# Small norm-parameter loads: one transfer per chunk in the list of later loads, in place of six or nine in one entry

## The chip, the cores and the metric

The kernel runs on one core of one Trainium2 chip (trn2). The metric is device time in microseconds (us), lower is better: the median of the timed executions. The change's time is measured against the kernel before on the same kind of chip. All data are float32.

## The reference

Two transformer layers run one after the other on `x` of 4 x 512 x 320 with a context of 4 x 1601 x 192. Each has self-attention, cross-attention to the context (20 heads of 16) and a gated feed-forward part (320 to 2 x 1280 and back). Each of the three parts begins with a layer norm that has its own scale `g` and bias `b` of 320 elements.

```python
def _ln(x, g, b):
    m = jnp.mean(x, axis=-1, keepdims=True)
    v = jnp.mean(jnp.square(x - m), axis=-1, keepdims=True)
    return (x - m) * jax.lax.rsqrt(v + EPS) * g + b
...
h1 = _ln(x, n1_g, n1_b)
x = _attn(h1, h1, q1, k1, v1, o1_w, o1_b, heads) + x
h2 = _ln(x, n2_g, n2_b)
x = _attn(h2, context, q2, k2, v2, o2_w, o2_b, heads) + x
h3 = _ln(x, n3_g, n3_b)
proj = h3 @ ff_w1 + ff_b1
a, g = jnp.split(proj, 2, axis=-1)
ff = a * jax.nn.gelu(g, approximate=False) @ ff_w2 + ff_b2
return ff + x
```

## The kernel before

**Units and chunks.** Attention is cut into units of one batch element and four heads: 20 units of self-attention and 20 of cross-attention in each layer, and then 4 feed-forward units. I count the attention units of the program from 0 to 79. A unit walks over its keys in chunks of 128: 4 chunks in a self unit, 13 in a cross unit. For every chunk and head, TensorE multiplies keys by queries in two passes (`st<-q,kT`, L1297), and in a third pass subtracts the row maximum (`st<-nrows,ones`, the same line). ScalarE takes the exponential (`pr`, L1307), and TensorE multiplies by the values (`av`, L1323). Beside this, the same rounds of TensorE compute scores of the next unit (`sps`, L1065), whose maxima VectorE reduces (`nmax` and `pm`, L1080).

**The row maxima travel by DMA.** When the maxima of the next unit are complete, `max_end` (from L1125) splits and transposes them on VectorE into `turned` (L1136), and four small transfers of 4 KB each (`nrows<-turned`, L1144) bring them into the rows that the third pass reads. In cross units these four are put on a list of errands and issued one round later. The first `st<-nrows,ones` product of the next unit can't start before all four have landed, and TensorE runs its instructions in order.

**Projections use staging buffers.** `both` (from L887) projects queries and keys of a self unit, ScalarE writes them to `low` (L913), GpSimd splits off `high` (L814, L815), and transfers at L863 move both into `kT` and `q`. There are two buffers `low`. A later unit's write to `low` waits until the transfers out of it are done.

**One DMA queue.** Apart from the first microseconds, every transfer is issued by SyncE (SP in the profile) in program order. An instruction that waits for an engine, or for one of eight semaphores that are used in turn, holds up all that stand behind it. The order of the queue follows from the Python order in which the kernel is written: a planner with rounds, due times and costs decides which projections, norms and errands run in which chunk.

**The list of later loads.** Weights for later parts are kept as closures in `loads`, a queue. At the end of each chunk of an attention unit one entry is taken out and run (`loads.popleft()()` at the end of `main`'s loop). What is left when a feed-forward unit begins is issued at once. The scales and biases of a norm come in columns of 128, 96 or 64 partitions with one element each (`load_columns`, L215 to L218, into `lng` and `lnb`): six transfers for the norms of the two attentions, eight for the third norm. `load_norm` issued them all in one entry, and the third norm's entry, `small`, had the feed-forward bias `b1` (L267) besides, nine in all.

Entries with such groups are put on the list at five places: for the second norm of layer 0 near the start, for the first norm of layer 1 in layer 0's cross-attention, for the third norm at unit 37 of layer 0, for the second norm of layer 1 after the first layer's feed-forward part, and for the third norm again at unit 77. A sixth group, the first norm of layer 0, is loaded at once by `now(load_self(0))` before the first unit.

Of the kernel before, what the change touches and what calls it, by code (L numbers as in the profile page):

```python
# [23 lines left out]
P = 128  # L24
# [11 lines left out]
HK = [(0, 0, P), (1, P, 96), (2, P + 96, 96)]  # L36
# [17 lines left out]
FK = [(0, 0, P), (1, P, P)]  # L54
REST = D - 2 * P
# [20 lines left out]
def kernel(ctx: ExitStack, tc: tile.TileContext, x, context, ws, out):  # L76
# [18 lines left out]
    nc = tc.nc  # L95
# [113 lines left out]
    def load_rows(t, w, chunks):  # L209
        return [  # L210
            lambda k=k, at=at, n=n: dma(out=t[:n, k], in_=w[at : at + n, :].rearrange("(k d) c -> d k c", d=SLOT))
            for k, at, n in chunks
        ]

    def load_columns(t, v, chunks):  # L215
        with nc.allow_non_contiguous_dma(reason="a vector's elements go to partitions"):
            for k, at, n in chunks:
                dma(out=t[:n, k : k + 1], in_=v[at : at + n].rearrange("(k d o) -> d k o", d=SLOT, o=1))  # L218

    def load_row(t, v):  # L220
        dma(out=t, in_=v.rearrange("(o d) -> o d", o=1).to_broadcast([P, D]))
# [5 lines left out]
            load_row(brow[(3 * l + i) % 2], ws[l][("o1_b", "o2_b", "ff_b2")[i]])  # L227

    def load_norm(l, i):
        for t, v in ((lng[i], ws[l][f"n{i + 1}_g"]), (lnb[i], ws[l][f"n{i + 1}_b"])):  # L230
            load_columns(t, v, FK if i == 2 else HK)
            if i == 2:
                for half in range(2):
                    load_columns(t[half * REST :], v, [(2, 2 * P, REST)])

    def load_self(l):
        return [lambda: load_norm(l, 0)] + [
            f for t, n in ((wq1, "q1"), (wk1, "k1"), (wv1, "v1")) for f in load_rows(t, ws[l][n], HK)
        ]

# [8 lines left out]
    def load_cross(l):  # L249
        def rows(t, w):  # L250
            return [
                lambda k=k: dma(out=t[:96, k], in_=w[k * 96 : (k + 1) * 96, :].rearrange("(k d) c -> d k c", d=32))
                for k in range(2)
            ]

        return (
            [lambda: load_norm(l, 1)]
            + load_rows(wq2, ws[l]["q2"], HK)
            + rows(wk2, ws[l]["k2"])
            + rows(wv2, ws[l]["v2"])  # L260
        )

    def load_ff(l):
        def small():
            load_norm(l, 2)
            with nc.allow_non_contiguous_dma(reason="a vector's elements go to partitions"):
                dma(out=b1, in_=ws[l]["ff_b1"].rearrange("(c p) -> p c", p=P))  # L267

        def last_rows(half):
            dma(  # L270
                out=room["w1r"][half * REST : (half + 1) * REST, :],
                in_=ws[l]["ff_w1"][2 * P :, half * FF : (half + 1) * FF].rearrange("(k d) f -> d k f", d=SLOT),
            )

        second = ws[l]["ff_w2"].rearrange("(c p) f -> p c f", p=P)
        return (
            [small],
            [lambda half=half: last_rows(half) for half in range(2)],
            [lambda c=c: dma(out=room["w2"][:, c], in_=second[:, c]) for c in range(NHC)],
        )  # L280
# [78 lines left out]
    at = 0  # L359
# [1174 lines left out]
    def before(u):  # L1534

        if u.kind == "cross" and u.g == 1 and u.b + 1 < B or u.kind == "self" and u.m == EARLY - 2:
            b = u.b + 1 if u.cross else 0
            if u.l == 0:
                load_context(b, 0)
                load_context(b, 1)  # L1540
                if u.cross:
                    add_turned(b, u.start + 46, 6)
        if u.kind == "self" and u.m == 0 and u.l:
            take_rooms(u.l)
        if u.kind == "cross" and u.m == B * G - 1:
            take_weights()
            loads.extend(load_first(u.l, (0, 1, 3)) + load_ff(u.l)[2])
        if u.kind == "cross" and u.m == B * G - 3:
            take_rests()
            small, rests, _ = load_ff(u.l)  # L1550
            loads.extend(small + rests)
        if u.kind == "cross" and u.m == B * G - 2:
            loads.extend(load_first(u.l, (4, 2)))
        if u.kind == "self" and u.m == EARLY:

            if u.l == 0:
                add_turned(0, u.start + 22, 2)
            add_context(0, lambda s: units[u.i - u.m + B * G].own.update(kv=s["cT"]), u.start + 36, yes)

    def after(u):  # L1560

        stage[u.b] += 1
        if u.b == B - 1:
            load_bias(u.l, ("self", "cross", "ff").index(u.kind) + 2)
            if u.kind == "self":
                loads.extend(load_out(u.l, "o2_w"))
            if u.kind == "cross" and u.l + 1 < L:
                loads.extend(load_out(u.l + 1, "o1_w"))
            if u.l + 1 < L:
                if u.kind == "ff":  # L1570
                    loads.extend(load_cross(u.l + 1))
                elif u.kind == "self":
                    loads.extend(load_self(u.l + 1))
# [82 lines left out]
    take_rooms(0)  # L1656
    now(load_x(0))
    now(load_self(0))
    load_bias(0, 0)
    load_bias(0, 1)  # L1660
# [27 lines left out]
    for fs in (load_out(0, "o1_w"), load_x(3), load_cross(0)):  # L1688
        loads.extend(fs)
# [11 lines left out]
    for i, u in enumerate(units):  # L1701
# [10 lines left out]
        for k in (3, SOON, AHEAD):  # L1712
            v = units[i + k] if i + k < len(units) else None
# [32 lines left out]
```

## Time and profile before

| what | value |
| --- | --- |
| median of 3 runs | 2952.94 us (2951.12 to 2955.01) |
| the profiled execution's own time | 2956.35 us |
| its span, first to last instruction | 2954.6 us |
| mean granted TensorE clock | 0.992 |
| TensorE busy, matmuls | 2872.8 us, 97% of the span |
| VectorE, ScalarE, GpSimd busy | 70%, 64%, 44% |
| transfers of L218 (`lng`, `lnb`) | 20 + 20, about 0.6 us of SP each |
| when the six groups start | 2.6, 97.8, 469.8, 1115.1, 1524.8, 2570.6 us |

The profiled execution took 3.41 us more than the median of the runs; 1.75 us of its time lie outside its span. Times in the views are from the start of the span. In a timeline row, the columns are start, busy time, engine, line, operation, output and inputs, shapes and count, and in brackets how long the engine was idle before it and who ended that. SPq is the issuing of SyncE: the time of such a row is that of issuing the transfers and of waits within it, not that of moving the data. PEclk is the granted TensorE clock as a share of full speed.

### The profile page before, as it was taken

The page shows a single profiled execution, that of the slowest core. Times are in us where ns is not written, and L with a number is a line of the kernel's source. Part 1 is how long each engine was busy: PE and PEld are TensorE (multiplying, and loading weights), DVE is VectorE, ACT ScalarE, POOL GpSimd, SP SyncE. Part 2 cuts the span into 40 slices and gives each one's busy share as a digit, 9 for nine tenths or more (in the row PEclk, how much of TensorE's full clock was granted, in tenths as well). Part 3 has the DMA queues.
Part 4 walks back from the last instruction along what each step waited for, and adds up shares of the span by engine and source line. Part 5 has one row for each costly group of instructions (what it writes and reads, how often), then busy time and mean ns, then how long its engine had stood idle before and what let it go on. Part 6 is the DMA issues. An engine that isn't in the chain of part 4 may idle for free.

```text
span 2954.6 us, 84378 instructions
## 1 busy us (share of the span) xinstructions
PE 2872.8 (97%) x35018; PEld 1514.5 (51%) x35018; DVE 2060.8 (70%) x4031; ACT 1890.9 (64%) x3754; POOL 1290.0 (44%) x1409
## 2 busy tenths in 40 slices
PE   8999999999999999999999999999999999999999
PEld 4445554555555555355554555555555555544554
DVE  7767887888888888323258778888888888873221
ACT  3766677887877878601138676778778788783000
POOL 3556344555545545211215663455455464461110
PEclk8999999999999999999999999999999999999999
DMA  4443224222232222210113342222221121222000
GB/s 105 107 121 101 71 65 107 55 71 71 53 89 57 52 62 62 70 31 11 42 43 82 98 105 68 63 62 54 55 65 46 50 71 43 58 54 79 20 22 14
DMA packets 186543, 188.70 MB, mean 64 GB/s; under 512 B 69668, under 2 KB 137264, under 8 KB 186160
## 3 DMA queue, kind: packets, MB, share of 16 engines
q1 hardware_dynamic: 185368, 182.11, 24.3%
q8 instruction: 276, 4.52, 0.6%
q10 hardware_dynamic: 760, 1.18, 0.2%
q14 instruction: 107, 0.88, 0.1%
q0 software_dynamic: 32, 0.00, 0.0%
HBM read 55.76 MB, written 29.36 MB: 29 GB/s over the span
## 4 chain that ended last, share of the span: by engine, by line
PE 81%; DVE 13%; DMA 2%; ACT 1%; SPq 1%; issue 1%; POOL 1%; ACTq 0%; POOLq 0%; DVEq 0%
PE av L1323 22%; PE st L1297 16%; PE fps L1408 9%; DVE pm L1080 8%; PE sps L1065 6%; PE yps L1515 6%; PE vps L1026 5%; PE ops L1223 3%; PE kps L962 3%; PE qkps L897 3%; DVE nmax L1080 3%; PE fps L1468 2%; PE qps L938 2%; PE sps L1092 1%; ACT pr L1307 1%
## 5 line engine op out<-in xcount | busy, mean ns | idle before, releaser
L1307 ACT ACTIVATE pr<-st 128x512 f32<-128x512 f32 (+1 forms) x2720 | 1404.8, 603 | 403.0 <-PE st L1297 367.8
L1080 DVE TENSOR_REDUCE pm<-sps 128x1 f32<-128x512 f32 x1920 | 1188.1, 681 | 149.9 <-PE sps L1065 138.1
L1343 POOL TENSOR_TENSOR o<-o,vo 128x512 f32<-128x512 f32 x576 | 740.2, 1285 | 966.7 <-ACT vo L1342 950.1
L1065 PE MATMUL sps<-kT,q 32*128 32x512 f32 x4800 | 868.6, 430 | 11.6 <-DMA q<-low 3.1
L1297 PE MATMUL st<-q,kT 32*128 32x512 f32 (+1 forms) x5120 | 782.9, 421 | 2.2 <-ACT low L913 1.9
L1323 PE MATMUL av<-pr,vals 128*32 128x512 f32 (+1 forms) x5440 | 737.2, 608 | 45.3 <-ACT pr L1307 9.7
L1297 PEld LDWEIGHTS st<-q,kT 32*128 32x128 f32 (+1 forms) x5120 | 417.4, 180 | 289.7 <-issue 122.0
L1297 PE MATMUL st<-nrows,ones 32*128 32x512 f32 (+1 forms) x2720 | 539.8, 399 | 12.0 <-DMA nrows<-turned 12.0
L1065 PEld LDWEIGHTS sps<-kT,q 32*128 32x128 f32 x4800 | 426.6, 184 | 91.7 <-ACT pr L1307 13.4
L1080 DVE TENSOR_REDUCE nmax<-sps 128x1 f32<-128x512 f32 x640 | 396.3, 681 | 101.8 <-PE sps L1065 97.1
L1342 ACT COPY vo<-av 128x512 f32<-128x512 f32 x576 | 352.6, 612 | 25.2 <-PE av L1323 21.1
L1479 ACT ACTIVATE gl<-fps,b 128x512 f32<-128x512 f32 x80 | 54.8, 687 | 414.2 <-PE fps L1468 303.3
L1408 PE MATMUL fps<-hT,w 128*128 128x512 f32 x640 | 283.0, 597 | 0.0
L1323 PEld LDWEIGHTS av<-pr,vals 128*32 128x32 f32 (+1 forms) x5440 | 111.2, 108 | 320.6 <-DVE pm L1080 181.3
L1297 PEld LDWEIGHTS st<-nrows,ones 32*128 32x128 f32 (+1 forms) x2720 | 245.2, 180 | 37.5 <-issue 9.9
L1480 DVE SCALAR_TENSOR_TENSOR hid<-fps,b,gl 128x512 f32<-128x512 f32 x80 | 59.7, 748 | 240.9 <-ACT gl L1479 238.9
L1408 PEld LDWEIGHTS fps<-hT,w 128*128 128x128 f32 x640 | 119.3, 190 | 155.3 <-issue 152.8
L1515 PE MATMUL yps<-w,hid 128*128 128x320 f32 x640 | 176.3, 435 | 0.1
L1515 PEld LDWEIGHTS yps<-w,hid 128*128 128x128 f32 x640 | 120.4, 190 | 56.5 <-ACT gl L1479 5.3
L1223 PEld LDWEIGHTS ops<-wo,aT 112*32 112x32 f32 (+1 forms) x3072 | 98.2, 110 | 58.3 <-issue 40.5
L1223 PE MATMUL ops<-wo,aT 112*32 112x160 f32 (+1 forms) x3072 | 125.0, 301 | 0.7 <-POOL aT L1205 0.7
L514 POOL TENSOR_SCALAR root<-root 128x4 f32<-128x4 f32 x22 | 5.2, 237 | 263.3 <-DVE root L508 262.6
(91 smaller groups left out, 2494.5 us busy)
## 6 DMA issues: line engine op xcount, KB each, us to landing
kT<-stages SPq DMA_DIRECT2D x160, 200.2 KB
oway<-o SPq DMA_DIRECT2D x80, 256.0 KB
q<-high SPq DMA_DIRECT2D x160, 64.0 KB
q<-low SPq DMA_DIRECT2D x160, 64.0 KB
kT<-high SPq DMA_DIRECT2D x60, 128.0 KB
q<-high SPq DMA_DIRECT2D x60, 128.0 KB
kT<-low SPq DMA_DIRECT2D x57, 128.0 KB
aT<-oway SPq DMA_DIRECT2D x32, 224.0 KB
```

The lines of the kernel that those rows point to most:

```text
L897: nc.tensor.matmul(ps[f : f + m, :w], lhsT=wqk[:n, k, f // GD, column : column + m], rhs=first.hT[:n, k, at : at + w], start=(k == 0), sto ...
L1026: nc.tensor.matmul(ps[f : f + m, :w], lhsT=u.kvT[:n, k, at + f : at + f + m], rhs=wv[:n, k, h0 * DH : h1 * DH], start=(k == 0), stop=(k == ...
L1065: nc.tensor.matmul(ps, lhsT=u.q[j * SLOT : (j + 1) * SLOT, e, t * P : (t + 1) * P], rhs=u.kT[j * SLOT : (j + 1) * SLOT, u.k0 + s * 512 : u ...
L1080: nc.vector.tensor_reduce(to[:, j : j + 1], ps, AX.X, ALU.max)
L1223: nc.tensor.matmul(ps[f : f + m, : D // 2], lhsT=aT[:n, k, f * NQ + t * SLOT : f * NQ + t * SLOT + m], rhs=wo[:n, k, cols], start=(k == 0) ...
L1297: nc.tensor.matmul(own[0][:r, :], lhsT=ones[rows, :r] if e == 2 else u.keys(rows, c), rhs=u.rows[rows, :] if e == 2 else u.q[rows, e, :], ...
L1307: nc.scalar.activation(p[:r], own[0][:r], AF.Exp)
L1323: nc.tensor.matmul(ps[j * SLOT : (j + 1) * SLOT, :], lhsT=columns_of[:r, head : head + SLOT], rhs=pr.pop((c, j))[:r, :], start=True, stop= ...
L1342: nc.scalar.copy(vo, ps)
L1343: nc.gpsimd.tensor_tensor(u.o, u.o, vo, ALU.add)
L1408: nc.tensor.matmul(ps, lhsT=w1[:, k, i * FF + c * P : i * FF + (c + 1) * P], rhs=natural(u.hT[:, k]), start=start, stop=stop,)
L1515: nc.tensor.matmul(ps[:, :D], lhsT=hid[c][:, t * P : (t + 1) * P], rhs=w2[:, c, :], start=(c == 0), stop=(c == NHC - 1),)
```

## The change

`load_columns` and `load_norm` no longer issue transfers but return lists of closures, one for each column. `load_self` and `load_cross` put these six entries ahead of the weights, and `load_ff` returns eight entries and a ninth for `b1`. So each group takes six or nine chunks in place of one, and every entry behind it on the list moves five or eight chunks later. No transfer is added or left out: SP has 1749 transfers in both. Line numbers behind the edited functions grow by up to 4.

```diff
     def load_columns(t, v, chunks):
-        with nc.allow_non_contiguous_dma(reason="a vector's elements go to partitions"):
-            for k, at, n in chunks:
+        def column(k, at, n):
+            with nc.allow_non_contiguous_dma(reason="a vector's elements go to partitions"):
                 dma(out=t[:n, k : k + 1], in_=v[at : at + n].rearrange("(k d o) -> d k o", d=SLOT, o=1))
 
+        return [lambda c=c: column(*c) for c in chunks]
...
     def load_norm(l, i):
+        fs = []
         for t, v in ((lng[i], ws[l][f"n{i + 1}_g"]), (lnb[i], ws[l][f"n{i + 1}_b"])):
-            load_columns(t, v, FK if i == 2 else HK)
+            fs += load_columns(t, v, FK if i == 2 else HK)
             if i == 2:
                 for half in range(2):
-                    load_columns(t[half * REST :], v, [(2, 2 * P, REST)])
+                    fs += load_columns(t[half * REST :], v, [(2, 2 * P, REST)])
+        return fs
 
     def load_self(l):
-        return [lambda: load_norm(l, 0)] + [
+        return load_norm(l, 0) + [
             f for t, n in ((wq1, "q1"), (wk1, "k1"), (wv1, "v1")) for f in load_rows(t, ws[l][n], HK)
         ]
...
         return (
-            [lambda: load_norm(l, 1)]
+            load_norm(l, 1)
             + load_rows(wq2, ws[l]["q2"], HK)
             + rows(wk2, ws[l]["k2"])
             + rows(wv2, ws[l]["v2"])
         )
...
     def load_ff(l):
-        def small():
-            load_norm(l, 2)
+        def biases():
             with nc.allow_non_contiguous_dma(reason="a vector's elements go to partitions"):
                 dma(out=b1, in_=ws[l]["ff_b1"].rearrange("(c p) -> p c", p=P))
...
         return (
-            [small],
+            load_norm(l, 2) + [biases],
```

On TensorE, VectorE, ScalarE and GpSimd every instruction keeps its place. Only SP's queue is reordered. Three places of it follow, in the order of the program.

The first is SP in self-attention of layer 0, near 98 us of the profile: `lng_121` and `lnb_124` are the second norm's parameters, `q_104` is the query buffer of a coming unit, `wq_113` the query weights of cross-attention. Before:

```order
L863 DMA q_104<-high 64x512
L863 DMA q_104<-low 64x512
L218 DMA lng_121<-in_L_xattn_n_g_dram 128x1x1
L218 DMA lng_121<-in_L_xattn_n_g_dram 96x1x1 x2
L218 DMA lnb_124<-in_L_xattn_n_b_dram 128x1x1
L218 DMA lnb_124<-in_L_xattn_n_b_dram 96x1x1 x2
L863 DMA q_104<-high 64x512
L863 DMA q_104<-low 64x512
L211 DMA wq_113<-in_L_xattn_q_dram 128x1x320
L1164 DMA oway_130<-o 4x32x512
L1144 DMA nrows_97<-turned 8x4x32 x4
```

And now:

```order
L866 DMA q_104<-high 64x512
L866 DMA q_104<-low 64x512
L218 DMA lng_121<-in_L_xattn_n_g_dram 128x1x1
L866 DMA q_104<-high 64x512
L866 DMA q_104<-low 64x512
L218 DMA lng_121<-in_L_xattn_n_g_dram 96x1x1
L1167 DMA oway_130<-o 4x32x512
L1147 DMA nrows_97<-turned 8x4x32 x4
L218 DMA lng_121<-in_L_xattn_n_g_dram 96x1x1
L218 DMA lnb_124<-in_L_xattn_n_b_dram 128x1x1
```

The second pair of `q_104` stands behind one small load, not six, and `wq_113` is no longer ahead of the four `nrows`.

The second place is SP in cross-attention of layer 0, near 470 us: `lng_120` and `lnb_123` are the first norm's parameters for layer 1, `nrows_97` the row maxima of unit 22. Before:

```order
L243 DMA wo<-in_L_xattn_o_w_dram 96x1x320
L752 DMA ctxT_127<-stages 768x1x64
L218 DMA lng_120<-in_L_xattn_n_g_dram 128x1x1
L218 DMA lng_120<-in_L_xattn_n_g_dram 96x1x1 x2
L218 DMA lnb_123<-in_L_xattn_n_b_dram 128x1x1
L218 DMA lnb_123<-in_L_xattn_n_b_dram 96x1x1 x2
L1144 DMA nrows_97<-turned 8x4x32 x4
L211 DMA wqk<-in_L_xattn_q_dram 128x1x320
L211 DMA wqk<-in_L_xattn_q_dram 96x1x320 x2
```

And now:

```order
L247 DMA wo<-in_L_xattn_o_w_dram 96x1x320
L755 DMA ctxT_127<-stages 768x1x64
L218 DMA lng_120<-in_L_xattn_n_g_dram 128x1x1
L1147 DMA nrows_97<-turned 8x4x32 x4
L218 DMA lng_120<-in_L_xattn_n_g_dram 96x1x1 x2
L218 DMA lnb_123<-in_L_xattn_n_b_dram 128x1x1
L1167 DMA oway_130<-o 4x32x512
L218 DMA lnb_123<-in_L_xattn_n_b_dram 96x1x1
```

One small load, not six, stands ahead of the four `nrows`.

The third place is SP in unit 37 of layer 0, from 1115 us on (the same in layer 1 from 2571 us): `w1r` are feed-forward weights, two transfers of 320 KB, and `nrows_97` the maxima of unit 38. Before:

```order
L218 DMA lnb_125<-in_L_xattn_n_b_dram 64x1x1 x2
L267 DMA b_117<-in_L_xattn_ff_b_dram 128x20x1
L1164 DMA oway_131<-o 4x32x512
L863 DMA kT_101<-stages 64x801 x4
L270 DMA w1r<-in_L_xattn_ff_w_dram 64x1x1280 x2
L863 DMA q_103<-high 64x256
L863 DMA q_103<-low 64x256
L863 DMA q_103<-high 64x256
L863 DMA q_103<-low 64x256
```

And now:

```order
L218 DMA lnb_125<-in_L_xattn_n_b_dram 64x1x1
L866 DMA q_103<-high 64x256
L866 DMA q_103<-low 64x256
L866 DMA q_103<-high 64x256
L866 DMA q_103<-low 64x256
L218 DMA lnb_125<-in_L_xattn_n_b_dram 64x1x1
L270 DMA b_117<-in_L_xattn_ff_b_dram 128x20x1
L273 DMA w1r<-in_L_xattn_ff_w_dram 64x1x1280 x2
L1147 DMA nrows_97<-turned 8x4x32 x4
```

The two `w1r` now stand directly ahead of the four `nrows` of unit 38; before, eight transfers of `q_103` lay between.

## The prediction

> **What bounds the kernel now.** I read the page first, to see which engine the whole time hangs on.
>
> ```profile
> PE 2872.8 (97%) x35018; PEld 1514.5 (51%) x35018; DVE 2060.8 (70%) x4031; ACT 1890.9 (64%) x3754; POOL 1290.0 (44%) x1409
> PE 81%; DVE 13%; DMA 2%; ACT 1%; SPq 1%; issue 1%; POOL 1%; ACTq 0%; POOLq 0%; DVEq 0%
> ```
>
> TensorE is busy for 97%, and the second row, the chain that ended last, is TensorE's for 81%. A change of the SP queue can only touch what TensorE waits for. So the next view is TensorE's waits, and in it one row is about transfers that L218 can hold up (columns: total us, times, longest us).
>
> ```profile
> PE st L1297 <- DMA nrows<-turned: 12.0, 10, 3.0
> ```
>
> The longest of these ten waits, 3.0 us, is at 478.78 us; TensorE's, VectorE's and SP's timelines show what led to it.
>
> ```profile
> 468.87 0.21 DVE L1136 STREAM_TRANSPOSE turned<-nmax 128x32 f32<-128x32 f32 x1
> ...
> 469.84 3.03 SPq L218 DMA_DIRECT2D lng<-in_L_xattn_n_g_dram  x3
> 472.92 1.89 SPq L218 DMA_DIRECT2D lnb<-in_L_xattn_n_b_dram  x3
> 474.90 2.67 SPq L1144 DMA_DIRECT2D nrows<-turned  x4
> ...
> 478.78 0.49 PE L1297 MATMUL st<-nrows,ones 32*128 32x512 f32 x2 [3.03 <-DMA nrows<-turned]
> ```
>
> The maxima of unit 22 were ready on VectorE at 469.08. SP was then issuing the six norm loads, from 469.84 to 474.81, and came to `nrows` only at 474.90. TensorE would have gone on at 478.78 - 3.03 = 475.75.
>
> The stall has a second price. The next view has TensorE's work and its granted clock in stretches that I cut at the clock's own changes (columns: length, busy time of PE, PEld, DVE, ACT, POOL, then PEclk, DMA share, GB/s).
>
> ```profile
> 169.10:172.50 3.40, 1.73 (x16) 0.46 (x16) 3.27 (x9) 1.77 (x4) 3.14 (x6) 1.00 0.56 147
> 476.31:479.72 3.41, 0.94 (x16) 0.59 (x18) 0.79 (x2) 0.44 (x1) 0.00 (x0) 1.00 0.18 50
> 479.72:486.55 6.83, 6.83 (x55) 2.88 (x56) 4.63 (x9) 4.26 (x9) 1.27 (x1) 0.50 0.26 61
> 1643.67:1647.08 3.41, 1.35 (x24) 0.67 (x20) 1.62 (x3) 0.89 (x3) 3.41 (x3) 1.00 0.46 119
> 1647.08:1650.49 3.41, 3.41 (x36) 1.76 (x38) 1.58 (x3) 2.13 (x5) 2.83 (x10) 0.50 0.86 224
> ```
>
> Behind a stretch of 3.41 us in which TensorE worked for only 0.94 us, the clock was 0.50 for 6.83 us, and TensorE was busy in all of it: 3.41 us of work at full clock took twice that. The rows near 1645 us show the same for 1.35 us of work, with one slow stretch. The row at 169 us, 1.73 us of work, was followed by full clock.
>
> A smaller stall lies behind the first group. These are rows of the chain of waits near 100 us, then ScalarE's and TensorE's timeline there.
>
> ```profile
> 97.75 0.60 SPq L218
> ...
> 101.01 0.60 SPq L218
> 101.65 1.18 SPq L863
> 102.88 2.38 DMA q<-low
> ...
> 105.37 0.47 ACT L913 ACTIVATE low<-qkps,scales 128x256 f32<-128x256 f32 x1 [1.87 <-DMA q<-low]
> 105.89 0.49 PE L1065 MATMUL sps<-kT,q 32*128 32x512 f32 x1 [0.88 <-ACT low L913]
> ```
>
> The six loads are on the chain: `q<-low` behind them empties a buffer that ScalarE wants to write, and TensorE waits 0.88 us for ScalarE.
>
> **The change part by part.** One small load costs SP about 0.60 us, 0.64 with the gap to the next:
>
> ```profile
> L218 SPq DMA_DIRECT2D lng<-in_L_xattn_n_g_dram x20: 592/602/1691, 2.6 to 2573.1; - x20
> ```
>
> *The group at 470 us.* One load, not six, stands ahead of `nrows`, which so move up by five issues, 5 x 0.64 = 3.2 us. The three loads at 469.84 took 3.03 us, not 1.9, so 1.1 us of the queue's own hold-up lies there; I leave it in front of `nrows`. The first `nrows` starts at 469.84 + 0.65 = 470.5, and the last is issued by 474.90 + 2.67 - 3.2 = 474.3. It lands 1.66 us after its issue begins, by this row of the chain:
>
> ```profile
> 476.99 1.66 DMA nrows<-turned
> ```
>
> So 476.99 - 3.2 + 1.66 = 475.4, ahead of the 475.75 at which TensorE is ready. The bounds: all 3.03 us saved, or, should the queue hold `nrows` another 1.1 us, 475.4 + 1.1 - 475.75 = 0.8 us left and 2.2 saved. I take 3.03, by the rows of the same queue. Even with 0.8 us idle, the stretch would keep more than the 1.73 us of work that was enough at 169 us, so the slow clock goes too: 6.83 x 0.5 = 3.41 us. Between nothing and 3.41, I take 3.41.
>
> *The group at 98 us.* `q<-low` stands behind one small load, and is issued about 3.2 us earlier, so its buffer is free at about 102 us, before ScalarE is ready at 105.37 - 1.87 = 103.5. The 0.88 us go. Lower bound 0: another operand could come next. I take 0.88.
>
> *The groups at 1115, 1525 and 2571 us* cost nothing now, and nothing is gained. Two rows of SP's timeline and one of the chain of waits show what covers them:
>
> ```profile
> 1120.21 0.59 SPq L267 DMA_DIRECT2D b<-in_L_xattn_ff_b_dram  x1
> 1123.13 0.61 SPq L1164 DMA_DIRECT2D oway<-o  x1
> ...
> 1519.05 12.05 DVE nmax L1080 x20
> ```
>
> At 1115 us the queue is done at 1120.80 and next waits for GpSimd's `o` until 1123.13, 2.3 us of cover; at 1525 us TensorE is held by VectorE's maxima for 12.05 us. The group at 2.6 us is issued by `now` and stays as it is.
>
> *Later weights.* Every weight behind a group comes five or eight chunks later. Two rows of the chain, a chunk apart, and the first users by source line and tile:
>
> ```profile
> 1112.68 1.07 PE av L1323 x8
> 1115.87 1.06 PE av L1323 x8
> ...
> L962 PE MATMUL kps<-w x1280: 330/332/357, 217.4 to 2362.9; 96*32 96x200 f32 x138, 96*32 96x201 f32 x45
> L938 PE MATMUL qps<-hT,wq x960: 377/379/382, 272.6 to 2592.3; 96*32 96x256 f32 x128, 128*32 128x256 f32 x64
> L1468 PE MATMUL fps<-hT,w1r x320: 589/589/693, 1232.0 to 2928.9; 64*128 64x512 f32 x160
> ```
>
> A chunk takes 3.2 us, so the delay is 16 to 26 us. The group at 98 us and the seven weight loads behind it are 13 entries, which end near 97.75 + 13 x 3.2 = 139 us; the key and query weights are first used at 217 and 273 us, `w1r` at 1232 us. Cost 0, since some 80 us cover it; without that cover, TensorE would wait for a weight as it did for `q<-low` above, some 2.4 us. SP issues as many transfers as before.
>
> The sum: 3.03 + 3.41 + 0.88 = 7.32 us. In the profiled execution's own terms 2956.35 - 7.32 = 2949.0. The median of the runs is 3.41 us below that execution; the same sum from it gives 2952.94 - 7.32 = **2945.6 us**.
>
> **The rivals.**
>
> *The slow clock isn't there to save.* The profiled execution lies 3.41 us above the median, just what 6.83 us at half clock cost. Other executions may cut the same 3.03 us of idleness into two stretches, each with more than 1.73 us of work, and keep full clock. Then only 3.03 + 0.88 = 3.91 us go: 2949.0 us. For it: the range of the three runs, 3.9 us, has room for such a spell. Against it: 3.03 us idle leave little room in two stretches of 3.41. The Trainium skill, page "TensorE: Matmul & The Clock Gate", section "Part 1: The HAM clock gate", says that half rate follows at least one idle window of about 3.4 us, and that the window runs free of the kernel's start. Read strictly, a gap of 3.03 us never fills a window, and the saving would be that of this rival; the row at 476.31, with 0.94 us of work and half clock behind it, differs, while a free phase fits a spell that is there in some runs only.
>
> *The stall only moves.* `nrows` could still be late at 478 us, if it is the queue's hold-up and not the issue count that delays it. Its price is at least the 0.8 us above; for a full stall the hold-up would have to grow from 1.1 to 4.3 us. Then 2952.9 - 0.9 = 2952 us.
>
> *Slower: `w1r` ahead of `nrows`.* In both layers, 640 KB now go directly ahead of the maxima of units 38 and 78.
>
> ```profile
> 1128.64 1.75 SPq L270 DMA_DIRECT2D w1r<-in_L_xattn_ff_w_dram  x2
> ...
> 1144.87 0.59 SPq L863 DMA_DIRECT2D q<-low  x1
> 1158.11 2.65 SPq L1144 DMA_DIRECT2D nrows<-turned  x4
> ...
> 1163.23 0.39 PE L1297 MATMUL st<-nrows,ones 32*128 32x512 f32 x1
> ```
>
> At the 224 GB/s of the row at 1647 us, 640 KB take 2.9 us, and their issue 1.75. If both fall directly ahead of 1158.11, `nrows` land 4.7 us later than now (issued by 1158.11 + 2.65 = 1160.8, landed 1.1 us behind the end of the last issue at 1161.9), that is at 1166.6, and TensorE, which uses them at 1163.23, waits 3.3 us and then loses 3.41 at half clock: 6.7 per layer, 13.4 in all, net +6.1 us, 2959.0. It decides from the point where SP comes to `w1r` later than 1158.1 - 4.7 = 1153.4. Against it: the small loads and `w1r` wait for no engine; SP is free from 1144.87 + 0.59 = 1145.5 to 1158.1. Three more small issues, 1.9 us, and `w1r` are done at 1149.2, and the data by 1152.1, 6 us ahead of need.
>
> **How the numbers follow.** The forecast has 0.56, the missing slow clock 0.25, the moved stall 0.07, the slower case 0.12. A measurement of this kernel can tell about 0.2%, 5.9 us. The forecast and little else is faster by more: 0.58. The slower case gives 0.12. The rest, 0.30, is within. The range: down to 2942.2, where one more slow spell of 3.41 us is gone; up to 2952.4, which takes in the case without the slow clock and a spell of 3.41 elsewhere.
>
> **What would show it.** In the profile of the changed kernel: `nrows` issued at 470 to 474 us and no wait of TensorE for them near 478; the clock at 1.00 from 476 to 487; no wait of ScalarE for `q<-low` near 105 us; `w1r` issued near 1140 to 1150 us and again in layer 1, with the `nrows` of units 38 and 78 not waited for. The prediction is wrong if a new stall of 2 us or more with a half clock behind it stands anywhere in place of the one at 478, or if `nrows` there are still late.

## The result and the profile after

| what | before | after |
| --- | --- | --- |
| median, 15 executions each | 2953.49 us (2950.87 to 2956.47) | 2946.70 us (2943.98 to 2953.61) |
| ratio | | 0.9982, interval 0.9976 to 0.9989 |
| span of the profiled execution | 2954.6 us | 2948.5 us |
| mean granted TensorE clock in it | 0.992 | 0.993 |

The change makes the kernel faster, by 3 to 7 us by the interval; the ratio stands for 5.3 us, the medians lie 6.8 us apart. The prediction was 2945.6 us, and the median is 1.1 us above it. First the page of the profile after, engine totals and the chain that ended last:

```profile
PE 2871.7 (97%) x35018; PEld 1513.0 (51%) x35018; DVE 2060.2 (70%) x4031; ACT 1890.3 (64%) x3754; POOL 1287.7 (44%) x1409
PE 81%; DVE 13%; ACT 1%; DMA 1%; issue 1%; POOL 1%; SPq 1%; POOLq 0%; ACTq 0%; DVEq 0%
```

TensorE is still the bound, with the same shares. In the list of TensorE's waits, the row that the prediction went by (total us, times, longest) is now:

```profile
PE st L1300 <- DMA nrows<-turned: 9.4, 9, 2.4
```

It was 12.0, 10, 3.0. One wait is gone, the longest. The timelines of VectorE, SP and TensorE show the place, unit 22. Its maxima come 3.6 us earlier in the span than before, by what happened ahead of this place, and its product 6.9 us earlier:

```profile
465.23 0.21 DVE L1139 STREAM_TRANSPOSE turned<-nmax 128x32 f32<-128x32 f32 x1
...
466.56 0.65 SPq L218 DMA_DIRECT2D lng<-in_L_xattn_n_g_dram  x1
467.31 2.69 SPq L1147 DMA_DIRECT2D nrows<-turned  x4
470.04 1.32 SPq L218 DMA_DIRECT2D lng<-in_L_xattn_n_g_dram  x2
...
471.92 0.39 PE L1300 MATMUL st<-nrows,ones 32*128 32x512 f32 x2
```

The maxima are turned at 465.23 + 0.21 = 465.44, one small load is issued, and `nrows` follow at 467.31, 1.9 us behind the maxima; before it was 474.90 - 469.08 = 5.8 us. (The prediction wanted to see `nrows` issued at 470 to 474 us; by the clock of the span they are earlier, because the whole unit is.) The last of the four is issued at 470.00, and TensorE uses them at 471.92 without a wait (no bracket behind the row). The other small loads come after `nrows`. The windows around the place (length, then busy time of PE, PEld, DVE, ACT, POOL, then the granted clock) hold full clock throughout:

```profile
464.00:476.00 12.00, 11.79 (x176) 6.27 (x168) 10.60 (x24) 9.82 (x21) 4.90 (x4) 1.00 0.24 55
476.00:487.00 11.00, 10.16 (x152) 5.27 (x156) 10.82 (x26) 8.36 (x19) 6.92 (x13) 1.00 0.54 133
```

The second place that the prediction named is the group at 98 us:

```profile
98.24 0.60 SPq L218 DMA_DIRECT2D lng<-in_L_xattn_n_g_dram  x1
98.89 0.61 SPq L866 DMA_DIRECT2D q<-high  x1
99.54 0.59 SPq L866 DMA_DIRECT2D q<-low  x1
...
104.42 0.47 ACT L916 ACTIVATE low<-qkps,scales 128x256 f32<-128x256 f32 x1 [0.44 <-PE qkps L900]
```

`q<-low` is issued at 99.54, 3.3 us earlier than before (102.88). ScalarE waits only 0.44 us, and for TensorE's product, not for a buffer. TensorE's wait of 0.88 us there is gone.

Third, the place of the slower rival, `w1r` ahead of the `nrows` of unit 38:

```profile
1140.33 2.23 SPq L273 DMA_DIRECT2D w1r<-in_L_xattn_ff_w_dram  x2
1151.23 2.63 SPq L1147 DMA_DIRECT2D nrows<-turned  x4
...
1156.37 0.39 PE L1300 MATMUL st<-nrows,ones 32*128 32x512 f32 x1
```

`w1r` is issued by 1142.6, 8.7 us ahead of `nrows`, and nobody waits for those. In layer 1 it is 2597.42 and 2607.59, the same.

**Where the time of the span went.** These are the stretches at half clock from 100 us to the last microsecond of the span, from the clock's own records (start and length in us):

| before | after |
| --- | --- |
| 203.2 (6.83), 479.7 (6.83), 1531.0 (6.83), 1647.1 (3.41) | 174.0 (3.41), 1064.9 (6.83), 1525.7 (3.41), 1648.5 (3.41) |
| 23.90 us in all | 17.06 us in all |

6.84 us less at half clock is 3.4 us of time, out of the 6.1 us between the spans. But it isn't the same list with one entry taken out: 479.7 is gone, and so is 203.2, while 174.0 and 1064.9 are new. (TensorE's waits ahead of these two, 1.85 and 1.53 us, are under the 2 us that the prediction named as a sign of being wrong.) Unit 8's wait for `nrows`, 1.88 us before and 1.85 after, brought half clock in the profile after only, at 174.0. So one profile beside another can't tell how large the clock's part is; the timed executions can, as below.

### The profile page after: what moved, and what is told of

Same layout as the page of the kernel before. It is cut to its first block, busy times and chain, and to the rows that moved or that the text cites. A ratio compares the mean times of both kernels' runs of the same rounds, so it can differ in the third digit from the quotient of the medians.

```text
span 2948.5 us, 84388 instructions
## 1 busy us (share of the span) xinstructions
PE 2871.7 (97%) x35018; PEld 1513.0 (51%) x35018; DVE 2060.2 (70%) x4031; ACT 1890.3 (64%) x3754; POOL 1287.7 (44%) x1409
## 4 chain that ended last, share of the span: by engine, by line
PE 81%; DVE 13%; ACT 1%; DMA 1%; issue 1%; POOL 1%; SPq 1%; POOLq 0%; ACTq 0%; DVEq 0%
PE av L1326 22%; PE st L1300 16%; PE fps L1411 10%; DVE pm L1083 8%; PE sps L1068 6%; PE yps L1518 6%; PE vps L1029 5%; PE ops L1226 3%; PE kps L965 3%; PE qkps L900 3%; DVE nmax L1083 3%; PE fps L1471 2%; PE qps L941 2%; PE sps L1095 1%; ACT pr L1310 1%
## 5 line engine op out<-in xcount | busy, mean ns | idle before, releaser
L1345 ACT COPY vo<-av 128x512 f32<-128x512 f32 x576 | 354.1, 615 | 23.9 <-PE av L1326 20.1
```

Of the source, the lines that this page charges most:

```text
L1345: nc.scalar.copy(vo, ps)
```

## The experiments

Eight runs, four in each of two sittings; seven are new kernels, the eighth is the changed kernel again. In both sittings the kernel before ran beside them: median 2953.38 us (35 executions) and 2953.28 us (30).

Each timed execution comes with its span and its mean granted clock, so that its time can be split: (1 - clock) x span is what the half clock cost, the rest is time less that. (The clock is given to 0.001, 2.9 us, in each execution, which averages out; idle time at half clock counts too. So does half clock in the first 100 us: there the ten traces have from 10.2 to 27.3 us of it, 5 to 14 us in this column, ahead of the first place at which any of these kernels differs.) Means with their standard errors, in us:

| kernel | executions | median | ratio to before (interval) | cost of half clock | rest |
| --- | --- | --- | --- | --- | --- |
| before | 65 | 2953.3 | | 20.5 (0.4) | 2933.4 (0.3) |
| after (15 and 10 of the last experiment) | 25 | 2946.6 | 0.9982, 0.9974 | 17.0 (0.8) | 2930.1 (0.4) |
| only the first norm's loads one by one | 11 | 2946.80 | 0.9981 (0.9972 to 0.9991) | 16.6 (1.1) | 2931.4 (0.8) |
| only the second norm's | 11 | 2953.19 | 1.0000 (0.9991 to 1.0009) | 22.3 (1.0) | 2931.4 (0.8) |
| only the third norm's | 12 | 2954.24 | 1.0009 (0.9998 to 1.0019) | 22.4 (1.6) | 2933.5 (0.5) |
| groups kept, rows first | 11 | 2950.16 | 0.9987 (0.9978 to 0.9997) | 19.6 (1.2) | 2930.9 (0.5) |
| group at 470 us doubled | 10 | 2960.60 | 1.0026 (1.0017 to 1.0035) | 25.2 (1.1) | 2935.7 (0.6) |
| group at 470 us in two halves | 11 | 2949.24 | 0.9987 (0.9979 to 0.9996) | 17.2 (0.9) | 2932.4 (0.8) |
| after, and rows first | 9 | 2946.25 | 0.9976 (0.9967 to 0.9986) | 15.7 (0.7) | 2930.7 (0.5) |
| after again | 10 | 2946.15 | 0.9974 (0.9965 to 0.9984) | 15.3 (1.4) | 2930.8 (0.7) |

The two columns don't follow the wait at unit 22 kernel by kernel, so I use them only where many executions stand behind them. Against the kernel before of the same sitting, the group in two halves has no wait there and yet a rest only 0.3 us lower (standard error 0.9); the kernel with only the second norm's loads one by one keeps the wait and has a rest 2.6 us lower (0.9); with the rows first, half clock costs only 0.8 us less (1.3).

### One kind of group alone

The changed kernel with two of the three groups put back into one entry. For the first norm alone:

```diff
-            load_norm(l, 1)
+            [lambda: now(load_norm(l, 1))]
...
-            load_norm(l, 2) + [biases],
+            [lambda: now(load_norm(l, 2) + [biases])],
```

> Only the group for the first norm of layer 1 (at 470 us) is spread; the other groups stay in one entry. My theory (the group held nrows of unit 22 back): TensorE's wait of 3.0 us at 478 is gone, and with it the slow clock that followed; 3.0 us less if that slow clock is only in some executions, up to 6.4 less if in all, so a ratio of 0.9978 to 0.9990. Rival (spreading relieves the queue at every group alike): about a fifth to a quarter of the change's 6.8 us, 1.5 us less, ratio 0.9995.

Measured: 2946.80 us, which is the whole gain as far as the intervals tell, though SP's order differs from the kernel before only between 470 and 525 us. TensorE's timeline and a window show no wait for the rows of unit 22 and full clock behind it; the wait near 105 us is still there, 0.95 us.

```profile
474.24 0.39 PE L1300 MATMUL st<-nrows,ones 32*128 32x512 f32 x2
```

```profile
468.00:488.00 20.00, 19.04 (x281) 9.79 (x284) 18.78 (x41) 15.85 (x34) 10.24 (x13) 1.00 0.38 89
```

For the second norm alone, the group at 98 us, the first and third are put back in the same way:

> Only the groups for the second norms (at 98 and 1525 us) are spread. Theory: ScalarE's wait for q<-low and TensorE's 0.88 us behind it at 105 us go, nothing else; the wait of 3.0 us at 478 stays; ratio 0.9997, between 0.9992 and 1.0003. Rival (relief at every group alike): two fifths of 6.8 us, 2.7 us less, ratio 0.9991, and it would need a second place of gain near 1525 us.

Measured: 2953.19 us, no gain that can be told from nothing (the interval reaches 2.7 us to both sides). ScalarE doesn't wait for `q<-low` near 105 us, as in the kernel after, so the small stall is gone, and what it cost is too little to be seen in the time. The stall of unit 22 is there in full; TensorE's timeline and two windows of this kernel:

```profile
475.77 0.79 PE L1300 MATMUL st<-nrows,ones 32*128 32x512 f32 x2 [3.34 <-DMA nrows<-turned]
```

```profile
471.49:474.90 3.41, 0.94 (x16) 0.30 (x8) 1.90 (x5) 0.33 (x1) 1.16 (x1) 1.00 0.08 4
474.90:485.14 10.24, 9.37 (x72) 4.15 (x76) 4.80 (x9) 4.92 (x10) 1.27 (x1) 0.50 0.24 61
```

Half clock lasts 10.24 us here, 9.37 of them with TensorE at work: a price of 4.7 us, not 3.4.

For the third norm alone:

> Only the groups for the third norms (at 1115 and 2571 us) are spread, so w1r stands directly ahead of nrows of units 38 and 78. Theory: no change within 0.5 us, ratio 1.0000 and between 0.9994 and 1.0006, nrows issued and landed as before. Rival (w1r delays nrows): TensorE waits 3 us for nrows near 1163 and 2619 us, 6 us or more slower. Rival (relief at every group alike): 2.7 us less.

Measured: 2954.24 us, no gain, and the wait at unit 22 is 2.86 us with 10.24 us at half clock. `w1r` are issued some 8.5 us ahead of the `nrows` of units 38 and 78, and TensorE doesn't wait for those, near 1163 and 2624 us of this span, so the rival with the late rows is out. That nothing changes within 0.5 us can't be told: the interval reaches from 0.6 us less to 5.6 us more, and four of the twelve executions took over 2959 us, against two of the 35 of the kernel before. The profile is one of these (span 2959.4). Windows near 2105 us:

```profile
2104.60:2108.01 3.41, 1.31 (x20) 0.71 (x20) 1.49 (x4) 0.98 (x3) 1.26 (x1) 1.00 0.03 6
2108.01:2114.84 6.83, 6.83 (x52) 2.75 (x48) 4.16 (x7) 4.06 (x8) 2.52 (x2) 0.50 0.07 10
```

Unit 66's wait for `nrows`, 1.39 us before, was 2.10 us here, and half clock followed. SP's order there is the same as in the kernel before, but the four `nrows` took it longer, 2.99 us before and 3.91 us here:

```profile
2102.64 2.99 SPq L1144 DMA_DIRECT2D nrows<-turned  x4
...
2101.74 3.91 SPq L1147 DMA_DIRECT2D nrows<-turned  x4
```

So this stretch isn't one that the edit reordered. Whether long executions are commoner in this kernel than in the kernel before stays open.

### The groups kept, the rows first

The kernel before, but in cross units no entry of the list is taken in the chunk between the maxima and the issue of their rows:

```diff
-            if loads:
+            if loads and (last or not (u.cross and nxt.cross) or c != u.nch - 3):
                 loads.popleft()()
```

> The kernel before, with all groups still in one entry, but no entry of the list is taken in the chunk between the maxima of a cross unit and the issue of their rows, so that the six loads at 470 us come behind nrows of unit 22. Theory: the same gain as spreading the group at 470 us alone, 3.0 to 6.4 us less, ratio 0.9978 to 0.9990, and no wait at 478. Rival (spreading itself helps): no gain, ratio 1.0000.

Measured: 2950.16 us. The six loads are still issued in one go, only behind `nrows`, and TensorE neither waits at unit 22 nor slows down near it. SP's timeline:

```profile
469.60 2.67 SPq L1144 DMA_DIRECT2D nrows<-turned  x4
472.31 1.94 SPq L218 DMA_DIRECT2D lng<-in_L_xattn_n_g_dram  x3
474.30 1.88 SPq L218 DMA_DIRECT2D lnb<-in_L_xattn_n_b_dram  x3
```

So the wait hangs on the place in the queue, not on the grouping, and the gain, 3.2 us by the medians, is at the low end of what I expected. That the median lies 3.4 us above that of the first experiment isn't explained with certainty, since the intervals overlap; but its profile shows a price of the group at 98 us that the prediction didn't have. SP's, ScalarE's and TensorE's timeline, then two windows:

```profile
98.89 2.64 SPq L218 DMA_DIRECT2D lnb<-in_L_xattn_n_b_dram  x3
...
104.71 0.47 ACT L913 ACTIVATE low<-qkps,scales 128x256 f32<-128x256 f32 x1 [3.02 <-DMA q<-low]
...
105.23 0.50 PE L1065 MATMUL sps<-kT,q 32*128 32x512 f32 x1 [2.05 <-ACT low L913]
```

```profile
102.25:105.66 3.41, 1.36 (x20) 0.72 (x16) 1.29 (x2) 0.95 (x3) 3.16 (x5) 1.00 0.58 134
105.66:109.07 3.41, 3.41 (x29) 1.01 (x28) 1.29 (x2) 2.05 (x5) 0.35 (x1) 0.50 0.35 104
```

The queue held up the group itself by some 0.7 us (2.64 in place of 1.9), TensorE waited 2.05 us in place of 0.88, and 3.41 us at half clock came behind it. It is one execution; whether it accounts for the median isn't shown.

### The count of loads ahead of the rows

Two kernels change only the number of small loads between the maxima of unit 22 and `nrows`. In one it is twelve, six of them into tiles that nothing reads:

```diff
-        return [lambda: load_norm(l, 0)] + [
+        def group():
+            load_norm(l, 0)
+            if l:
+                for t, n in zip(spare, ("n1_g", "n1_b")):
+                    load_columns(t, ws[l][n], HK)
+
+        return [group] + [
```

> The kernel before, with the group at 470 us doubled: six more small loads of the same size behind the six, into spare tiles that nothing reads. Theory (nrows of unit 22 stand behind the group in one queue, 0.64 us per transfer): nrows are issued 6 x 0.64 = 3.8 us later, at about 478.7, TensorE's wait at 478 grows from 3.0 to about 6.9 us, and the granted clock is 0.50 behind it for one spell of 6.83 us or more. Time by the idle part alone +3.8 us, about 2957; with a longer half clock up to +7 us, about 2960. Rival (the queue's own hold-up of 1.1 us and not the count sets the delay): the wait grows by less than 1.5 us and the time stays within 2 us of before. Rival (TensorE's wait is filled by work that would be idle elsewhere): the wait grows but the time doesn't.

In the other it is three, scales and biases being two entries:

```diff
-        return [lambda: load_norm(l, 0)] + [
+        pair = ((lng[0], "n1_g"), (lnb[0], "n1_b"))
+        return [lambda t=t, n=n: load_columns(t, ws[l][n], HK) for t, n in pair] + [
```

> The kernel before, with the group at 470 us in two entries of three loads (the scales in one chunk, the biases in the next), so that three small loads stand ahead of nrows of unit 22 in place of six or one. Theory (count of issues): nrows move up by 3 x 0.64 = 1.9 us, TensorE's wait at 478 falls from 3.0 to about 1.1 us. TensorE then works for about 0.9 + 1.9 = 2.8 us of a stretch of 3.41 us, more than the 1.73 us that kept full clock at 169 us, so no half clock stands near 480 us: 1.9 + 3.4 = 5.3 us less than before, about 2948. If the loss to the clock only follows the length of the wait, it is 1.9 us and a part of 3.4, about 2950. Rival (what delays nrows is the queue's hold-up of 1.1 us within the first three loads and a wait for a semaphore): the wait stays at 2 us or more with half clock behind it, 2952.

Measured with twelve: 2960.60 us. SP's and TensorE's timeline, then the windows:

```profile
471.54 1.94 SPq L219 DMA_DIRECT2D lng<-in_L_xattn_n_g_dram  x3
473.53 2.66 SPq L219 DMA_DIRECT2D lnb<-in_L_xattn_n_b_dram  x3
476.24 1.88 SPq L219 DMA_DIRECT2D spare<-in_L_xattn_n_g_dram  x3
478.17 1.88 SPq L219 DMA_DIRECT2D spare<-in_L_xattn_n_b_dram  x3
480.14 2.67 SPq L1151 DMA_DIRECT2D nrows<-turned  x4
...
484.13 0.80 PE L1304 MATMUL st<-nrows,ones 32*128 32x512 f32 x2 [6.57 <-DMA nrows<-turned]
```

```profile
480.92:484.13 3.21, 0.00 (x1) 0.03 (x1) 0.00 (x0) 0.00 (x0) 0.00 (x0) 0.50 0.05 5
484.13:491.16 7.03, 7.03 (x56) 3.36 (x56) 3.26 (x7) 3.28 (x7) 1.27 (x1) 0.50 0.21 62
```

The wait grew from 3.03 to 6.57 us, by 3.5 for six issues, as the count says (3.8). Half clock behind it with TensorE at work is 7.03 us against 6.83: no more than before. By this the time should rise by some 3.6 us; it rose by 7.3. Of the other 3.7 us the table puts 3.1 on half clock (25.2 - 20.5 = 4.7, less 1.6 for the 3.21 idle us above); where in the span that lies stays open, and the half clock of the first 100 us is in that column too.

With three: 2949.24 us. SP's and TensorE's timeline:

```profile
467.68 1.94 SPq L218 DMA_DIRECT2D lng<-in_L_xattn_n_g_dram  x3
469.72 2.67 SPq L1145 DMA_DIRECT2D nrows<-turned  x4
...
473.35 0.39 PE L1298 MATMUL st<-q,kT 32*128 32x512 f32 x1
...
473.58 0.45 PE L1298 MATMUL st<-nrows,ones 32*128 32x512 f32 x2
```

I had expected a wait of 1.1 us; there is none. Three loads took 1.94 us here, where the first three of the kernel before took 3.03: the hold-up of 1.1 us didn't come. The clock near 480 us is full. For 1, 3, 6 and 12 loads ahead of `nrows` the wait is 0, 0, 3.03 and 6.57 us, and the medians are 2946.2, 2949.2, 2953.3 and 2960.6. The step between the first two isn't one of this wait: the kernel with one load is the whole change, and the intervals of the two overlap. With no wait and no half clock left here, 3.03 + 3.41 = 6.4 us should have gone; 4.0 us did, and why the rest didn't stays open.

### The change and the rows first; the change again

The changed kernel with the condition of the rows-first kernel added:

> The changed kernel, and besides no entry of the list of later loads is taken in the chunk of a cross unit between its row maxima and the issue of their rows. Theory: the stall at 478 is gone already, so nothing is left for the second edit: the time of the changed kernel, 2946 to 2948, no wait for nrows of unit 22, and the wait at 105 us absent as in the changed kernel. Rival (weights ahead of nrows delay them elsewhere too): another 1 to 4 us less, 2943 to 2946, with smaller waits for nrows of units 8 and 48.

Measured: 2946.25 us, beside 2946.15 for the changed kernel in the same sitting. Its profile has no wait for `nrows` longer than 1.1 us, and still the time isn't another. None of the kernels tried is faster than the change.

> The changed kernel once more, for a second profile and more executions with their clocks. Theory (the idle part and the half clock behind 478 us are both gone in every execution): the time less what the clock cost, that is time - (1 - clock) x span, lies 4 us under the kernel before, and the mean clock is higher by about 0.001, which is 3 us; together 6 to 7 us, about 2946.5, with no wait and no half clock near 478 us in the profile. Rival (the half clock behind 478 us is there in some executions only): the mean clock is that of the kernel before within 0.0003, and 4 us in all are saved, about 2949.5.

Measured: 2946.15 us, the time that I expected; but against the kernel before of the same sitting half clock costs 5.4 us less (standard error 1.5) and the rest is 2.0 us lower (0.8), where I expected 3 and 4. The rival, with no gain from the clock, is out; the split is not the one expected. SP's timeline and a window at unit 22 show what the first profile showed:

```profile
465.57 0.65 SPq L218 DMA_DIRECT2D lng<-in_L_xattn_n_g_dram  x1
466.32 2.83 SPq L1147 DMA_DIRECT2D nrows<-turned  x4
```

```profile
464.00:487.00 23.00, 21.98 (x324) 11.46 (x320) 21.69 (x50) 18.20 (x39) 12.19 (x18) 1.00 0.36 88
```

The half clock near 1065 us, which was new in the first profile after, is not in this one.

## Why the prediction was right

**The wait at 478 us (3.03 us): right.** Place and size held. `nrows` start 1.9 us behind the maxima, and no wait is left. In four kernels with six or more loads ahead of `nrows` the wait is there (3.03, 3.34, 2.86 and 6.57 us); in six with three, one or none it isn't. Where the prediction was too careful: it left the queue's hold-up of 1.1 us in front of `nrows` and had them ready 0.35 us before need; they moved up by 3.9 us against the maxima, not 3.2. The hold-up isn't tied to these loads; it is 1.1, 0.7 or nothing for the same transfers in different executions. Its cause is open. It isn't a wait for one of the eight semaphores: in the trace of the kernel before, the transfer that had used the held load's semaphore last had landed some 3 us before that load's issue began.

**The half clock behind it (3.41 us): the mechanism was right, against the rival to which I gave the next largest chance; the size came from one execution.** In all four traces with the full wait, half clock stands there (6.83, 10.24, 10.24 and 10.24 us); in none of the six without it is there any from 464 to 487 us. With TensorE at work in 6.83, 9.37, 9.56 and 7.03 us of it, the price was 3.4, 4.7, 4.8 and 3.5 us; the prediction had sized it by the lowest of these. Over all executions the table gives 20.5 - 17.0 = 3.5 us for the clock (standard error 0.9) and 2933.4 - 2930.1 = 3.3 us for the rest (0.5), where the prediction had 3.41 and 3.91. The rival would have had 0 and 3.91. That both parts agree this well with the forecast is partly luck, since the last experiment alone gives 5.4 and 2.0. The Trainium skill, page "TensorE: Matmul & The Clock Gate", section "Part 1: The HAM clock gate", asks for at least one idle window of about 3.4 us; the traces differ, since half clock came behind a window with 0.94 us of work. That the window runs free agrees: half clock began 0.94 us after TensorE went on in the kernel before, and 0.87 us before it in the second experiment.

**The wait at 105 us (0.88 us): its mechanism is shown, its gain isn't.** The wait is in all six traces that keep that group (0.74 to 0.95 us, and 2.05 once) and in none of the four that spread it. Done alone it moves the time by nothing that can be measured.

**The groups at 1115, 1525 and 2571 us, and the later weights: no gain, as forecast.** The third norm's loads alone gave 1.0009, and TensorE waits for no weight in any of the ten traces. (The 2.4 us that the prediction gave for such a wait are the time of the transfer `q<-low`; TensorE's own wait there was 0.88.)

**The slower rival fell at its own condition.** It needed `w1r` to be issued less than 4.7 us ahead of `nrows`; they are 8.7 us ahead, as the prediction had argued from the time in which SP is free.

**A bound that was reasoned badly.** The prediction took 1.73 us of work in a stretch of 3.41 as enough for full clock, from one row. It isn't a threshold. Three windows of the profile after:

```profile
1645.10:1648.51 3.41, 2.22 (x32) 1.06 (x28) 1.64 (x5) 1.26 (x3) 3.41 (x6) 1.00 0.32 103
1648.51:1651.92 3.41, 3.41 (x28) 1.27 (x32) 1.16 (x2) 1.75 (x4) 1.18 (x2) 0.50 0.21 40
1634.86:1638.27 3.41, 1.73 (x16) 0.46 (x16) 3.06 (x5) 1.71 (x4) 3.20 (x5) 1.00 0.32 90
```

A stretch with 2.22 us of work was followed by half clock, one with 1.73 us wasn't. It did no harm because the wait went altogether; with 0.8 us of it left, the 3.41 us would not have been safe.

**The total.** The forecast had 7.32 us less than a median of three executions, and 6.8 us came, from 15. Of the 7.32, the 0.88 us can't be seen in any measured time, and the 3.41 us come from one spell, so a forecast within 1.1 us is closer than its terms are known.

## What to carry to other kernels

In a queue that issues in program order, what counted here was how many transfers stood between the moment a small, urgent transfer became ready and its own issue; a batch of tiny loads cost 0.64 us each there in this kernel, and nothing that could be measured at the places where no engine waited for what stood behind it. Spreading the batch and moving it behind the urgent transfer both removed the wait. A gap of 3 us on TensorE was paid for about twice here, once idle and once at half clock, so the longest gaps are the ones to look at first.

## What the runs showed of the hardware

After the first 100 us, half clock came in lengths of 3.41, 6.83 and 10.24 us, on a grid of 3.41 us whose phase differs between executions. I counted TensorE's work in the windows of that grid in all ten traces. After a window with at most 1.50 us of work, half clock followed 16 times of 16; after one with 1.60 to 2.40 us, 11 times of about 30. So a stall of 1 to 2 us costs half clock in some executions and not in others. It is one source of the scatter around a median: in 35 executions of the kernel before the mean clock went from 0.996 to 0.991, which is 15 us of time. Another is the first 100 us, in which half clock took 23.9 us in the traces before and after, but 10.2 in two of the others and 27.3 in one, with the same order of instructions.

In all ten traces there is half clock near 1525 us (1542 with the group doubled), behind a window in which TensorE shows 3.0 to 3.2 us of busy time. What sets it off there was not tried.
